# Row sums through the right matrix in groups of eight, with the output products eleven turns behind a row's first stage

## The chip, the cores and the metric

The kernel runs on one core of a Trainium2 chip. The metric is the device time of one execution in microseconds (us). The engines are TensorE (PE; its weight loads are listed apart as PEld), VectorE (DVE), ScalarE (ACT), GpSimd (POOL) and SyncE (SP), which here only issues transfers. Everything is in 32-bit floats.

## What is computed

The input x has 384 x 384 positions of 128 channels. Two layers follow each other; the first mixes rows, the second works row by row. Cut to what matters:

```
# layer 0
z     = layernorm(x)
left  = (z @ Wl + bl) * sigmoid(z @ Wlg + blg)
right = (z @ Wr + br) * sigmoid(z @ Wrg + brg)
core  = einsum('bikh,bjkh->bijh', left, right)
x1    = x + sigmoid(x @ Wg + bg) * (layernorm(core) @ Wout + bout)
# layer 1
left  = x1 @ W_left + b_left + x1 @ W_eq + b_eq
gate  = sigmoid(x1 @ W_gate + b_gate)
rsum  = sum over j of (x1 @ W_right + b_right)      # one vector of 128 per row i
out   = layernorm((left * rsum * gate) @ W_out + b_out + x1)
```

The sum over j and the product with W_right can change places. So the kernel adds up each row of x1 first (one vector of 128 per row) and sends only these sums through W_right. It also multiplies rsum into W_out, which gives each row an output matrix of its own.

## The kernel before

It works in three stages. Stage 1 normalises x, forms left and right and writes them to memory. Stage 2 forms core, channel by channel. Stage 3 begins with the first transposes at about 1888 us and does the end of layer 0 and all of layer 1, one row i of 384 positions at a time. Only stage 3 is touched.

In stage 3 the channels lie on the 128 partitions and the 384 positions of a row along the free dimension. The order on every engine is the order in which the program writes the instructions (`seq` keeps it)[...]. The main loop runs over turns t (L610 to L644). In each turn different functions work on different rows, so that each engine finds its inputs ready:

- `front(f)` (L488) runs ahead. It forms the gate gT of row f-2 (matmul "pg" L493, sigmoid on ACT L495), and every fourth row asks for the x of four rows by a transfer, 16 rows ahead (L499). At the start it is up to 14 rows ahead of t, later 2. For the first 24 rows x is transposed on TensorE ("pxt" L506); after that it is put together in a tile "xt" by two transfers (L441, and an accumulating one that POOL issues, L449).
- `load_core` (L622) asks for core and its scaling for four rows, eight rows ahead; `scale_core(t)` (L627) multiplies them on POOL into "cs".
- `last(t-10)` (L629) multiplies by the layer norm's weight on DVE (L601) and adds its bias on POOL (L602).
- `right_sums(m)` (L631) is called in every fourth turn, t = 6, 10, 14 and so on, for rows 4m to 4m+3: one matmul "pq" (L514) of W_right with a tile "tot" of 128 x 4, which holds four rows' sums, and the addition of the bias on DVE into "rsum" (L516).
- `layer0(t-2)` (L633) is a row's first stage: matmul "pr" (L530), then two DVE instructions (L531, L533). The second writes x1T and, on the side, the row's sum into its column of "tot".
- `out_matrix(t-6)` (L635): ACT scales W_out by a column of rsum into "wo" (L541).
- `gated_left(t-3)` (L637): matmuls "pg" (L547) and "pl" (L548), sigmoid on ACT (L550), product "u" on DVE (L552).
- `layer1(t-7)` and `stats1(t-7)` (L639): the output product "py", three times a matmul of u with wo (L559) and a transpose of x1T added into it (L560); its statistics on DVE (L574, L576). After every second row POOL turns the statistics of two rows into a scale and a shift (L578 to L583).
- `norm1(t-9)` (L642) normalises on ACT (L590), and every fourth turn `store` (L644) writes four rows out.

After the loop L646 to L663 finish the last four rows.

The TensorE order in a turn is therefore: pg (and pxt) of `front`, pq in every fourth turn, pr, the gate and left products, py. Results of TensorE go into PSUM banks: four of them, taken in rotation by pr, pq, pg, pl and pxt (`bank`), and four more for py. The x1T and u tiles have 7 buffers each (pool "p3l", L616), the x tiles 7 of four rows each (pool "p3x", L416).

Of the kernel before, what the change touches and what calls it, by code (L numbers as in the profile page):

```python
# [8 lines left out]
F32 = mybir.dt.float32  # L9
AF = mybir.ActivationFunctionType  # L10
ALU = mybir.AluOpType
# [3 lines left out]
P = 128  # L15
# [4 lines left out]
def triangle_then_gated_row_kernel(ctx: ExitStack, tc: tile.TileContext, a: dict, out: bass.AP):  # L20
# [12 lines left out]
    nc = tc.nc  # L33
    x = a["x"].rearrange("b i j c -> (b i) j c")
    y = out.rearrange("b i j c -> (b i) j c")
    N, _, C = x.shape
# [7 lines left out]
    RG = 4  # L44
    A = 14
# [10 lines left out]
    def seq(ins):  # L56

        return tc.keep_in_program_order(ins)
# [21 lines left out]
    with ExitStack() as ctx2:  # L80
        lrp = ctx2.enter_context(tc.tile_pool(name="lr", bufs=2))
        inp = [ctx2.enter_context(tc.tile_pool(name="p2in", bufs=2))]
# [13 lines left out]
        with tc.tile_pool(name="p1x", bufs=6, side="right") as xp, \  # L96
# [74 lines left out]
            def after(kind, name):  # L171

                shape, view = ([P, 1], "(p o) -> p o") if kind == "col" else ([P, P], None)
                t = const(shape, kind + "_" + name)
                later.append((t, a[name].rearrange(view, o=1) if view else a[name]))
                return t
# [6 lines left out]
            wright, bright = after("mat", "L1_conv_W_right"), after("col", "L1_conv_b_right")  # L183
# [67 lines left out]
            def front(n, q, z):  # L251

                pt = tps.tile([P, 4, P], F32, tag="pt", name="pt")
                for r in range(4):
                    seq(nc.tensor.transpose(pt[:, r, :], z[:, r, :], ident))
                zt = zts[n, q] = ztp.tile([P, 4, P], F32, tag="zt", name="zt")
                seq(nc.scalar.copy(zt, pt))  # L257
# [101 lines left out]
        with tc.tile_pool(name="p2more", bufs=1, side="right", reuse_waits="tile") as more, \  # L359
# [10 lines left out]
            right = {}  # L370
# [15 lines left out]
            for h in range(H):  # L386
                fill(h + 1)
                t, rr = loaded2.pop(h), right.pop(h)
                pc = ps.tile([P, NB, 512], F32, tag="pc", name="pc")
                for kb in range(NB):  # L390
                    for ib in range(NB):
                        seq(nc.tensor.matmul(  # L392
                            pc[:, ib, :N], lhsT=t[:, kb, ib * P:(ib + 1) * P, 0], rhs=rr[:, kb],
                            start=(kb == 0), stop=(kb == NB - 1),
# [17 lines left out]
    with ExitStack() as ctx3:  # L412
        def pool(name, bufs, **kw):
            return ctx3.enter_context(tc.tile_pool(name=name, bufs=bufs, reuse_waits="tile", **kw))

        xp, fp, inp, op = pool("p3x", 7), pool("p3f", A + 4), pool("p3in", 3), pool("p3out", 3)  # L416
        wp, sp, late = pool("p3w", 4), pool("p3s", 4), []
        ps, ps2 = pool("p3ps", 4, space=PSUM), pool("p3ps2", 4, space=PSUM)

        def bank(name):  # L420
            return ps.tile([P, 512], F32, tag="bank", name=name)

        def work(name, pool=wp):
            return pool.tile([P, N], F32, tag=name, name=name)
# [4 lines left out]
        rows, yts, pair, quad, xin, xts, cin = {}, {}, {}, {}, {}, {}, {}  # L429
# [24 lines left out]
        def load_core(i0):  # L454
            if i0 < N:
                ct = inp.tile([P, RG, N], F32, tag="ct", name="ct")
                seq(nc.sync.dma_start(out=ct, in_=core_d[i0:i0 + RG].rearrange("i h j -> h i j")))
                rt = inp.tile([P, RG, N], F32, tag="rt", name="rt")
                seq(nc.sync.dma_start(
                    out=rt.rearrange("p i j -> p (i j)"),  # L460
                    in_=rstd_d[i0:i0 + RG].rearrange("i j -> (i j)").partition_broadcast(P),
                ))
                cin[i0] = ct, rt
# [19 lines left out]
                seq(nc.vector.scalar_tensor_tensor(r, r, 1.5, m, ALU.add, ALU.mult))  # L483
                seq(nc.gpsimd.dma_start(out=rstd_d[b * P:(b + 1) * P, :], in_=r))

        D = 10

        def front(f):  # L488

# [17 lines left out]
                    seq(nc.scalar.copy(xT, pxt[:, :N]))  # L507
                rows[f] = {"xT": xT}

        def right_sums(m):  # L510

            q = quad[m]
            pq = bank("pq")
            seq(nc.tensor.matmul(pq[:, :4], lhsT=wright, rhs=q["tot"], start=True, stop=True))  # L514
            q["rsum"] = sp.tile([P, 4], F32, tag="rsum", name="rsum")
            seq(nc.vector.tensor_scalar(q["rsum"], pq[:, :4], bright, None, ALU.add))  # L516

        def scale_core(i):
            ct, rt = cin[i // RG * RG]
# [3 lines left out]
        def layer0(i):  # L523

            r = rows[i]
            m, n = divmod(i, 4)
            if n == 0:
                quad[m] = {"tot": sp.tile([P, 4], F32, tag="tot", name="tot")}
            pr = bank("pr")
            seq(nc.tensor.matmul(pr[:, :N], lhsT=wc, rhs=r["cs"], start=True, stop=True))  # L530
            seq(nc.vector.scalar_tensor_tensor(pr[:, :N], pr[:, :N], bz, r["gT"], ALU.add, ALU.mult))  # L531
            x1T = r["x1T"] = work("x1T", late[0])
            seq(nc.vector.scalar_tensor_tensor(  # L533
                x1T, pr[:, :N], bout1, r["xT"], ALU.add, ALU.add, accum_out=quad[m]["tot"][:, n:n + 1]
            ))

        def out_matrix(i):

            wo = rows[i]["wo"] = wp.tile([P, C], F32, tag="wo", name="wo")
            m, n = divmod(i, 4)  # L540
            seq(nc.scalar.activation(wo, wout1, AF.Copy, scale=quad[m]["rsum"][:, n:n + 1]))  # L541

        def gated_left(i):
# [10 lines left out]
        def layer1(i, py):  # L554

            r = rows[i]
            r["py"] = py
            for s in cols:
                seq(nc.tensor.matmul(py[:, s], lhsT=r["u"][:, s], rhs=r["wo"], start=True, stop=False))  # L559
                seq(nc.tensor.matmul(  # L560
                    py[:, s], lhsT=r["x1T"][:, s], rhs=ident, start=False, stop=True, is_transpose=True
                ))

        def stats1(i):

            py = rows[i]["py"]
            m, n = divmod(i, 2)
            if n == 0:
                pair[m] = [sp.tile(s, F32, tag=k, name=k) for k, s in
                           (("mv", [P, 2, NB, 2]), ("rs", [P, 2, NB]), ("nm", [P, 2, NB]))]  # L570
            mv, rs, nm = pair[m]
            st = sp.tile([P, NB, 6], F32, tag="st", name="st")
            for b in range(NB):
                seq(nc.vector.bn_stats(st[:, b, :], py[:, cols[b]]))  # L574
            for b in range(NB):
                seq(nc.vector.bn_aggr(mv[:, n, b, :], st[:, b, :]))  # L576
            if n == 1:
                seq(nc.gpsimd.tensor_scalar(rs, mv[:, :, :, 1], EPS, 1.0, ALU.add, ALU.mult))  # L578
                seq(nc.gpsimd.tensor_tensor(  # L579
                    rs, rs, mhalf[:, :2 * NB].rearrange("p (a b) -> p a b", b=NB), ALU.pow  # L580
                ))
                seq(nc.gpsimd.tensor_tensor(nm, mv[:, :, :, 0], rs, ALU.mult))
                seq(nc.gpsimd.tensor_scalar(rs, rs, -1.0, 0.0, ALU.mult, ALU.add))  # L583

        def norm1(i):
            m, n = divmod(i, 2)
            mv, rs, nm = pair[m]
            py = rows[i]["py"]
            for b, s in enumerate(cols):
                seq(nc.scalar.activation(  # L590
                    py[:, s], py[:, s], AF.Identity, bias=nm[:, n, b:b + 1], scale=rs[:, n, b:b + 1]
                ))

        def last(i):

            i0, n = i // RG * RG, i % RG
            if n == 0:
                yts[i] = op.tile([P, RG, NB, C], F32, tag="yt", name="yt")
            yt = yts[i0][:, n]
            py = rows.pop(i)["py"]  # L600
            seq(nc.vector.tensor_tensor(yt, py[:, :N].rearrange("p (b c) -> p b c", b=NB), lnsb, ALU.mult))  # L601
            seq(nc.gpsimd.tensor_tensor(yt, yt, lnbb, ALU.add))  # L602

        def store(i0):
            seq(nc.sync.dma_start(out=y[i0:i0 + RG].rearrange("i (b p) c -> p i b c", p=P), in_=yts.pop(i0)))
# [4 lines left out]
        for t in range(N + 3):  # L610

            while f < min(N + 2, t + max(2, A - t // 3)):
                if f == 6:
                    rstd()
                    end2.close()
                    late.append(pool("p3l", 7, side="right"))  # L616
                    load_core(0)
                    load_core(RG)
                front(f)
                f += 1  # L620
            if t % RG == 0:
                load_core(t + 2 * RG)  # L622
            if added <= f + 8:
                add_x(added)
                added += RG
            if t < N:
                scale_core(t)  # L627
            if t >= D:
                last(t - D)  # L629
            if t >= 6 and (t - 6) % 4 == 0:  # L630
                right_sums((t - 6) // 4)  # L631
            if 2 <= t < N + 2:
                layer0(t - 2)  # L633
            if t >= 6:
                out_matrix(t - 6)  # L635
            if t >= 3:
                gated_left(t - 3)  # L637
            if t >= 7:
                layer1(t - 7, ps2.tile([P, 512], F32, tag="py", name="py"))  # L639
                stats1(t - 7)  # L640
            if t >= 9:
                norm1(t - 9)  # L642
            if t >= D and (t - D) % RG == RG - 1:
                store(t - D - RG + 1)  # L644

        for i in range(N - 3, N):  # L646
            out_matrix(i)
# [45 lines left out]
```

## Time and profile before

The time before is 3333.22 us, the median of 3 runs (3332.3 to 3334.1). The profiled execution spans 3331.8 us with a mean granted TensorE clock of 0.996. The costliest groups of stage 3, over the whole run:

| line | engine | what | count | busy us | mean ns of one |
|---|---|---|---|---|---|
| L559 | PE | py, u with wo, 128 columns | 2304 | 403.0 | 275 |
| L530 | PE | pr, 384 columns | 768 | 318.9 | 497 |
| L560 | PE | py, transpose of x1T | 1152 | 314.0 | 273 |
| L548 | PE | pl, 384 columns | 768 | 311.6 | 488 |
| L547 | PE | pg of the gate, 384 columns | 768 | 311.4 | 487 |
| L590 | ACT | normalise py | 1152 | 494.3 | 429 |
| L521 | POOL | cs | 384 | 405.0 | 1059 |
| L602 | POOL | yt | 384 | 403.9 | 1052 |

The profile counts two TensorE instructions for each 32-bit matmul with its weight load and one for each transpose, so 384 rows give 768 pr and 2304 py. The records of neighbouring matmuls overlap, so their busy times add up to more than the time that they take. A line of the timeline gives the start of a run of instructions, how long it lasts, engine, line, operation, what is written and read, shapes, and how many there are; the brackets at its end give the engine's idle time before it and who ended it.

### The profile page before, as it was taken

How to read it: one execution, taken by the hardware profiler on the slowest of the kernel's cores; microseconds unless marked ns; L12 is line 12 of the kernel's file. 1: busy time of each engine (PE TensorE's matmuls, PEld its weight loads, DVE VectorE, ACT ScalarE, POOL GpSimd, SP SyncE). 2: the span in 40 equal slices, each digit the busy share in tenths (PEclk: the TensorE clock that was granted, in tenths of full speed). 3: DMA queues.
4: the chain of work that ended last, by engine and by line, in shares of the span. 5: the costliest groups of instructions: out<-in, count | busy, mean ns of one | idle time of the engine just before them, and what ended most of it. 6: DMA issues, size and time to landing. Idle time of an engine off the chain costs nothing.

```text
span 3331.8 us, 48534 instructions
## 1 busy us (share of the span) xinstructions
PE 3283.0 (99%) x12584; PEld 2004.5 (60%) x12584; DVE 2503.8 (75%) x8074; ACT 1949.2 (59%) x4049; POOL 2250.2 (68%) x3267
## 2 busy tenths in 40 slices
PE   8999999999999999999999999999999999999997
PEld 4444444444444566666666567777777777777775
DVE  6777777777777655555555678888888888888887
ACT  4455555555555433333334467777777777777776
POOL 5555555555555465565566468888888888888887
PEclk9999999999999999999999999999999999999999
DMA  5899899999999498998999988889888988988883
GB/s 148 245 282 281 253 282 275 260 281 269 266 281 263 149 282 283 284 282 282 284 282 284 277 257 249 271 274 275 266 272 273 272 269 273 276 268 270 273 269 95
DMA packets 924619, 872.93 MB, mean 262 GB/s; under 512 B 24868, under 2 KB 839720, under 8 KB 924344
## 3 DMA queue, kind: packets, MB, share of 16 engines
q1 hardware_dynamic: 904960, 794.32, 76.2%
q0 software_dynamic: 13152, 71.37, 10.5%
q10 hardware_dynamic: 6232, 4.13, 0.4%
q8 instruction: 103, 1.69, 0.2%
q14 instruction: 172, 1.41, 0.1%
HBM read 507.85 MB, written 361.89 MB: 261 GB/s over the span
## 4 chain that ended last, share of the span: by engine, by line
PE 62%; ACT 1%; POOL 1%; DVE 0%; issue 0%; DMA 0%; POOLq 0%; SPq 0%; ACTq 0%
PE pc L392 22%; PE pr L530 7%; PE py L559 7%; PE pg L493 7%; PE pl L548 7%; PE pg L547 7%; PE py L560 4%; ACT py L590 1%; POOL rs L579 0%; PE pq L514 0%; DMA xt<-nd_d 0%; POOL yt L602 0%; PE pxt L506 0%; DVE yt L601 0%; DVE st L574 0%
## 5 line engine op out<-in xcount | busy, mean ns | idle before, releaser
L291 PE MATMUL pr<-wz,zt 128*128 128x512 f32 x2304 | 1042.8, 594 | 0.7 <-ACT zt L257 0.7
L298 ACT ACTIVATE sg<-pr,rs 128x256 f32<-128x256 f32 x1152 | 482.8, 470 | 507.8 <-PE pr L291 375.1
L392 PE MATMUL pc<-rr,lrh 128*128 128x384 f32 x2304 | 743.3, 486 | 1.9 <-DVE lr L300 1.9
L300 DVE SCALAR_TENSOR_TENSOR lr<-pr,rs,sg 128x256 f32<-128x256 f32 x1152 | 504.8, 480 | 274.8 <-ACT sg L298 226.9
L291 PEld LDWEIGHTS pr<-wz,zt 128*128 128x128 f32 x2304 | 415.3, 191 | 412.5 <-issue 346.9
L392 PEld LDWEIGHTS pc<-rr,lrh 128*128 128x128 f32 x2304 | 452.0, 196 | 293.2 <-issue 2.5
L590 ACT ACTIVATE py<-py,nm,rs 128x128 f32<-128x128 f32 x1152 | 494.3, 429 | 184.4 <-POOL rs L583 90.8
L559 PEld LDWEIGHTS py<-wo,u 128*128 128x128 f32 x2304 | 377.5, 191 | 102.4 <-ACT wo L541 1.7
L401 DVE TENSOR_TENSOR csum<-csum,ct 128x1152 f32<-128x1152 f32 x128 | 180.6, 1411 | 343.0 <-ACT ct L398 343.0
L521 POOL TENSOR_TENSOR cs<-ct,rt 128x384 f32<-128x384 f32 x384 | 405.0, 1059 | 2.8 <-PE pr L530 2.6
L398 ACT COPY ct<-pc 128x1152 f32<-128x1152 f32 x128 | 143.2, 1118 | 450.5 <-PE pc L392 450.5
L602 POOL TENSOR_TENSOR yt<-yt,lnb 128x384 f32<-128x384 f32 x384 | 403.9, 1052 | 2.9 <-DVE yt L601 2.6
L559 PE MATMUL py<-wo,u 128*128 128x128 f32 x2304 | 403.0, 275 | 1.2 <-ACT wo L541 1.2
L378 POOL COPY rr<-lrh 128x768 f32<-128x768 f32 x128 | 184.8, 1444 | 298.6 <-DMA lrh<-lr_d 287.4
L574 DVE BATCH_NORM_STATS2 st<-py 128x6 f32<-128x128 f32 x1152 | 266.1, 286 | 96.0 <-PE py L560 95.3
L246 POOL TENSOR_TENSOR z<-xt,nd 128x512 f32<-128x512 f32 x288 | 299.8, 1041 | 43.4 <-POOL z L246 30.0
L530 PE MATMUL pr<-cs,wc 128*128 128x384 f32 x768 | 318.9, 497 | 5.4 <-POOL cs L521 5.4
L236 POOL TENSOR_SCALAR sd<-mv 128x8 f32<-128x8 f32 x144 | 28.4, 197 | 436.5 <-DVE mv L225 436.4
L560 PE MATMUL py<-ident,x1T 128*128 128x128 f32 x1152 | 314.0, 273 | 0.0
L548 PE MATMUL pl<-x1T,mat_L_conv_W_left 128*128 128x384 f32 x768 | 311.6, 488 | 1.2 <-ACT gT L495 1.2
L547 PE MATMUL pg<-x1T,mat_L_conv_W_gate 128*128 128x384 f32 x768 | 311.4, 487 | 1.0 <-DVE x1T L533 0.6
L493 PE MATMUL pg<-xt,mat_L_conv_Wg 128*128 128x384 f32 x720 | 292.0, 487 | 0.0
(96 smaller groups left out, 4919.6 us busy)
## 6 DMA issues: line engine op xcount, KB each, us to landing
lr_d<-lr SPq DMA_DIRECT2D x128, 1024.0 KB, 7.2
lrh<-lr_d SPq DMA_DIRECT2D x128, 768.0 KB, 7.7
xt_d<-zt SPq DMA_DIRECT2D x288, 256.0 KB, 5.5
ct<-core_d SPq DMA_DIRECT2D x96, 768.0 KB, 6.4
rt<-rstd_d SPq DMA_DIRECT2D x96, 768.0 KB, 8.1
out_dram<-yt SPq DMA_DIRECT2D x95, 768.0 KB, 4.9
core_d<-ct SPq DMA_DIRECT2D x125, 576.0 KB, 8.6
xt<-in_x_dram SPq DMA_DIRECT2D x140, 512.0 KB, 6.8
```

The lines of the kernel that those rows point to most:

```text
L291: seq(nc.tensor.matmul(pr[:, r, :], lhsT=zts[n, q][:, 2 * half + r, :], rhs=wz, start=True, stop=True))
L298: seq(nc.scalar.activation(sg[r], pr[:, r, 2 * H:], AF.Sigmoid, scale=rs[r]))
L300: seq(nc.vector.scalar_tensor_tensor(t[:, :, c * XR + r0 + r, :], pr[:, r, :2 * H].rearrange("k (h s) -> k h s", s=2), rs[r], sg[r].rearra ...
L392: seq(nc.tensor.matmul(pc[:, ib, :N], lhsT=t[:, kb, ib * P:(ib + 1) * P, 0], rhs=rr[:, kb], start=(kb == 0), stop=(kb == NB - 1),))
L493: seq(nc.tensor.matmul(pg[:, :N], lhsT=wg0, rhs=r["xT"], start=True, stop=True))
L521: seq(nc.gpsimd.tensor_tensor(cs, ct[:, i % RG], rt[:, i % RG], ALU.mult))
L530: seq(nc.tensor.matmul(pr[:, :N], lhsT=wc, rhs=r["cs"], start=True, stop=True))
L547: seq(nc.tensor.matmul(pg2[:, :N], lhsT=wgate, rhs=r["x1T"], start=True, stop=True))
L548: seq(nc.tensor.matmul(pl[:, :N], lhsT=wleft, rhs=r["x1T"], start=True, stop=True))
L559: seq(nc.tensor.matmul(py[:, s], lhsT=r["u"][:, s], rhs=r["wo"], start=True, stop=False))
L560: seq(nc.tensor.matmul(py[:, s], lhsT=r["x1T"][:, s], rhs=ident, start=False, stop=True, is_transpose=True))
L590: seq(nc.scalar.activation(py[:, s], py[:, s], AF.Identity, bias=nm[:, n, b:b + 1], scale=rs[:, n, b:b + 1]))
```

## The change

The row sums are now sent through W_right eight rows at a time, by a matmul of 128 x 8, so that there are fewer of these small matmuls. The first row of a group then has to wait for seven more rows before its rsum exists, so everything from `out_matrix` on moves from seven turns behind to eleven. In the last 48 rows the groups are of four, and at rows 337, 345, 353 and 361 one row joins the turn of the row ahead of it, so that the output products are seven turns behind again at the end and the code after the loop stays as it is. A table made ahead of the loop holds the group of each row (`group`), the turns in which sums are formed (`sums`) and the turn of each row's output product (`turn`, `at`). The x1T and u tiles get 11 buffers in place of 7 to live longer, and the x tiles 6 in place of 7, which makes room for them.

```diff
-        xp, fp, inp, op = pool("p3x", 7), pool("p3f", A + 4), pool("p3in", 3), pool("p3out", 3)
+        xp, fp, inp, op = pool("p3x", 6), pool("p3f", A + 4), pool("p3in", 3), pool("p3out", 3)
...
-        D = 10
+        firsts = list(range(0, N - 48, 8)) + list(range(N - 48, N, 4))
+        group, sums, turn = {}, {}, []
+        for i0, i1 in zip(firsts, firsts[1:] + [N]):
+            sums[i1 + 2] = i0, i1
+            for i in range(i0, i1):
+                group[i] = i0, i - i0
+                t = turn[-1] + 1 if i else 0
+                turn.append(max(i1 + 3, t - (i0 >= N - 48 and i % 8 == 1 and t > i + 7)))
+        assert turn[N - 5:] == list(range(N + 2, N + 7))
+        at = {t: [i for i in range(N) if turn[i] == t] for t in range(N + 7)}
...
-            seq(nc.tensor.matmul(pq[:, :4], lhsT=wright, rhs=q["tot"], start=True, stop=True))
-            q["rsum"] = sp.tile([P, 4], F32, tag="rsum", name="rsum")
-            seq(nc.vector.tensor_scalar(q["rsum"], pq[:, :4], bright, None, ALU.add))
+            seq(nc.tensor.matmul(pq[:, :i1 - i0], lhsT=wright, rhs=q["tot"][:, :i1 - i0], start=True, stop=True))
+            q["rsum"] = sp.tile([P, 8], F32, tag="rsum", name="rsum")
+            seq(nc.vector.tensor_scalar(q["rsum"][:, :i1 - i0], pq[:, :i1 - i0], bright, None, ALU.add))
...
-                    late.append(pool("p3l", 7, side="right"))
+                    late.append(pool("p3l", 11, side="right"))
...
-            if t >= D:
-                last(t - D)
-            if t >= 6 and (t - 6) % 4 == 0:
-                right_sums((t - 6) // 4)
+            done = at.get(t - 3, [])
+            for i in done:
+                last(i)
+            if t in sums:
+                right_sums(*sums[t])
             if 2 <= t < N + 2:
                 layer0(t - 2)
-            if t >= 6:
-                out_matrix(t - 6)
+            for i in at[t + 1]:
+                if i < N - 3:
+                    out_matrix(i)
             if t >= 3:
                 gated_left(t - 3)
-            if t >= 7:
-                layer1(t - 7, ps2.tile([P, 512], F32, tag="py", name="py"))
-                stats1(t - 7)
-            if t >= 9:
-                norm1(t - 9)
-            if t >= D and (t - D) % RG == RG - 1:
-                store(t - D - RG + 1)
+            for i in at[t]:
+                layer1(i, ps2.tile([P, 512], F32, tag="py", name="py"))
+                stats1(i)
+            for i in at.get(t - 2, []):
+                norm1(i)
+            for i in done:
+                if i % RG == RG - 1:
+                    store(i - RG + 1)
```

More of the change, by code (lines that the diff above doesn't have):

```diff
@@ L508, in front, with right_sums @@
                 rows[f] = {"xT": xT}
-        def right_sums(m):
-            q = quad[m]
+        def right_sums(i0, i1):
+            q = quad[i0]
             pq = bank("pq")
-            seq(nc.tensor.matmul(pq[:, :4], lhsT=wright, rhs=q["tot"], start=True, stop=True))
-            q["rsum"] = sp.tile([P, 4], F32, tag="rsum", name="rsum")
-            seq(nc.vector.tensor_scalar(q["rsum"], pq[:, :4], bright, None, ALU.add))
+            seq(nc.tensor.matmul(pq[:, :i1 - i0], lhsT=wright, rhs=q["tot"][:, :i1 - i0], start=True, stop=True))
+            q["rsum"] = sp.tile([P, 8], F32, tag="rsum", name="rsum")
+            seq(nc.vector.tensor_scalar(q["rsum"][:, :i1 - i0], pq[:, :i1 - i0], bright, None, ALU.add))
         def scale_core(i):
@@ L525, in layer0 @@
             r = rows[i]
-            m, n = divmod(i, 4)
+            m, n = group[i]
             if n == 0:
-                quad[m] = {"tot": sp.tile([P, 4], F32, tag="tot", name="tot")}
+                quad[m] = {"tot": sp.tile([P, 8], F32, tag="tot", name="tot")}
             pr = bank("pr")
@@ L539, in out_matrix @@
             wo = rows[i]["wo"] = wp.tile([P, C], F32, tag="wo", name="wo")
-            m, n = divmod(i, 4)
+            m, n = group[i]
             seq(nc.scalar.activation(wo, wout1, AF.Copy, scale=quad[m]["rsum"][:, n:n + 1]))
```

## The prediction, on record before the changed kernel ran

> **What bounds the kernel now.** I read the page's engine shares first, then the busy time of the third stage alone, TensorE's waits in it, and TensorE's timeline over two turns. A turn is one pass of the loop over t; "pr" of one turn to "pr" of the next is its length. The page's part 1 and chain by engine:
>
> ```profile
> PE 3283.0 (99%) x12584; PEld 2004.5 (60%) x12584; DVE 2503.8 (75%) x8074; ACT 1949.2 (59%) x4049; POOL 2250.2 (68%) x3267
> ...
> PE 62%; ACT 1%; POOL 1%; DVE 0%; issue 0%; DMA 0%; POOLq 0%; SPq 0%; ACTq 0%
> ```
>
> TensorE is busy for 99% and holds nearly all of what the chain names. The third stage, which alone is changed, runs from 1913.4 us (first pr) to the end. Busy time in its even part:
>
> ```profile
> core 0: us, PE busy (x) PEld busy (x) DVE busy (x) ACT busy (x) POOL busy (x), PEclk, DMA share, GB/s
> 1960.00:3300.00 1340.00, 1338.80 (x6456) 948.15 (x6455) 1178.10 (x4160) 977.21 (x2210) 1146.38 (x1567) 1.00 0.87 263
> ```
>
> PE idles 1.2 us in 1340; DVE is busy 88%, POOL 86%, ACT 73%, the transfers 87%. TensorE's waits from 1960 to 3304 us are one line (waiter, whom for, us in all, times, longest):
>
> ```profile
> PE pl L548 <- ACT gT L495: 1.2, 2, 0.6
> ```
>
> So here TensorE's own queue is the time, and an instruction taken off it shortens the stage, if it cost its queue anything. The small product pq (right_sums, L514) has its own view:
>
> ```profile
> L514 PEld LDWEIGHTS pq<-tot,mat_L_conv_W_right x192: 186/190/192, 1928.6 to 3305.4; 128*128 128x128 f32 x192
> L514 PE MATMUL pq<-tot,mat_L_conv_W_right x192: 169/248/253, 1928.7 to 3305.4; 128*128 128x4 f32 x192
> L516 DVE TENSOR_SCALAR rsum<-pq,col_L_conv_b_right x96: 210/211/214, 1929.1 to 3307.8; 128x4 f32<-128x4 f32 x96
> ...
>   ACT wo L541: 26.0, 94
> ```
>
> It runs 96 times, each as two weight loads and two matmuls (min/median/max ns). Only ScalarE's wo waits for it. Its cost is not the 248 ns record; it is what it adds between starts. TensorE's timeline, a turn without pq and the next one with it (start, us, line):
>
> ```profile
> 2604.76 0.81 PE L493 MATMUL pg<-xt,mat_L_conv_Wg 128*128 128x384 f32 x2
> 2605.41 0.81 PE L530 MATMUL pr<-cs,wc 128*128 128x384 f32 x2
> 2606.05 0.81 PE L547 MATMUL pg<-x1T,mat_L_conv_W_gate 128*128 128x384 f32 x2
> ...
> 2607.34 0.38 PE L559 MATMUL py<-wo,u 128*128 128x128 f32 x2
> ...
> 2608.34 0.81 PE L493 MATMUL pg<-xt,mat_L_conv_Wg 128*128 128x384 f32 x2
> 2608.99 0.28 PE L514 MATMUL pq<-tot,mat_L_conv_W_right 128*128 128x4 f32 x2
> 2609.13 0.89 PE L530 MATMUL pr<-cs,wc 128*128 128x384 f32 x2
> 2609.86 0.81 PE L547 MATMUL pg<-x1T,mat_L_conv_W_gate 128*128 128x384 f32 x2
> 2611.14 0.38 PE L559 MATMUL py<-wo,u 128*128 128x128 f32 x2
> ```
>
> py to py is 2607.34 - 2603.77 = 3.57 us without pq and 2611.14 - 2607.34 = 3.80 us with it. It splits in two: pq to pr is 0.14 us, and pr to the next product 0.73 instead of 0.64. Over the stage I took pr to pr of all turns: median 3.578 us in 272 turns without pq at their end, 3.717 us in 90 with one (+0.139), and 3.66 us in the turn that begins behind one (+0.083). **One pq costs 0.222 us of TensorE's queue**, four columns wide.
>
> [...] records of 0.81 us start every 0.645 us. So I count starts. [...] In the trace the pair before pq loads under the 384-column matmul before it; pq's four columns are too short to cover the two loads that follow. Hence the cost is loads without cover, and eight columns should cost about the same.
>
> **The change part by part.**
>
> *Fewer pq.* The rows are grouped in eights up to row 336 (42 groups) and in fours to 384 (12): 54 pq in place of 96. 42 x 0.222 = 9.3 us off TensorE's queue, all on the path. Rsum on DVE goes 42 times by 0.21 us, off the path.
>
> *Wider pq.* A 384-column matmul starts its successor 322 ns later, 0.84 ns a column; 4 columns x 2 matmuls x 42 x 0.84 = 0.3 us at most, zero if covered by the loads. I take 0.3.
>
> *Lag 11 in place of 7.* Each row's py, stats, norm, last and store keep their distances among themselves and move four turns back. x1T and u get 11 buffers instead of 7, so a buffer is written again two turns after py read it, as before (t = i+13 against i+11). Nothing new to wait for. The pq stands one turn behind the last x1T of its group, as before.
>
> *Start.* Turns 7 to 10 lose their py set (2608.34 - 2607.34 = 1.00 us each), which is run later. That costs nothing if TensorE stays full without it. Two such turns can be seen in the trace: the one from 1928.87 took 2.99 us, just its products plus the 0.08 behind a pq; the one from 1926.37 (without pg) took 2.50 where its products and pq sum to 2.07, an excess of 0.42. Bounds: 0 and all four sets, 4.0 us. I take 0.6.
>
> *Four double turns.* To come back from lag 11 to 7, turns 347, 354, 361 and 368 carry two rows' py: 1.00 us more TensorE work in each, the same sets that the start left out. DVE then has two rows' stats (+1.0 us on 3.16, below TensorE's 4.58). Two turns on ACT has six norms: 0.73 x 3.58 = 2.6, plus 1.35, is 3.97 us in a turn of 3.58. Queued behind on ACT are the next gT and g2; DVE's u, its next pr and x1T wait for them, and TensorE's next gate product waits for x1T. Three turns on DVE has a second yt (+0.56) and POOL too (+1.06). Between x1T and the gate product that reads it the trace shows 1.2 us (x1T begun 3301.27 and done near 3301.9; product 3303.07), about what the later norm takes. Bounds: 0, and a full 1.0 us each, 4.0. I take 0.2 each, 0.8. py has four PSUM buffers; the second py of a double turn needs the yt of the same turn, which DVE runs first (3300.15 to 3300.71, py at 3301.43): no wait.
>
> *Six x tiles in place of seven.* Tile f+16 is asked for in turn f-1 and its buffer was last read by row f-5's layer0 in turn f-3. The issue waits at SP, with core loads and stores queued behind, only if DVE is over two turns late. The core loads stand eight turns ahead (28.6 us) of a landing of 6.4 to 8.1 us (page, part 6). Early, where front runs ahead, one load (row 48) is asked for a turn before its buffer is free; the core load behind it keeps seven turns. Cost 0, hidden by that lead.
>
> *Fewer late banks.* The one wait of TensorE above comes in turns with a pq, which takes a bank out of four, so pl needs the bank of the same turn's pg, whose gT was late:
>
> ```profile
> 1986.92 0.57 ACT L495 ACTIVATE gT<-pg,col_L_conv_bg 128x384 f32<-128x384 f32 x1
> ...
> 1987.55 0.91 PE L548 MATMUL pl<-x1T,mat_L_conv_W_left 128*128 128x384 f32 x2 [0.56 <-ACT gT L495]
> ```
>
> Two turns (4.49 from 1985.5, 4.57 from 2027.4) are 0.83 and 0.91 us above 3.66. With half the pq there I count half: -0.9.
>
> *The end* keeps its order: the last rows are in fours at lag 7.
>
> Sum: -9.3 + 0.3 + 0.6 + 0.8 - 0.9 = -8.5; 3333.2 - 8.5 = **3324.7 us**.
>
> **The rivals.**
> 1. *More comes off*: start and doubles cost nothing and both late banks go: -9.3 - 1.7 = 3322.2. For it: PE has hardly a wait. Against: the excess of 0.42 at the start is real.
> 2. *The moved work isn't free*: turns 7 to 10 run at the pace of the chain cs, pr, x1T (TensorE idles 2.0 and 3.3 us for cs at 1913 and 1921), and doubles stall 0.5 us each: -9.3 + 4.0 + 2.0 = 3329.9. Against: from turn 5 on the trace has no such wait for cs.
> 3. *Slower*: with transfers at 87%, and one x tile less, SP issues late and 96 core loads each hold up cs and TensorE by 0.2 us, +19.2: 3333.2 - 9.3 + 19.2 = 3343. Against: the eight turns of lead. Only a wait at SP longer than 20 us would show.
>
> **How the numbers follow.** Forecast 0.70 (3323.3 to 3326.5); rival 1, 0.10; rival 2, 0.14 (3326.5 to 3331); rival 3, 0.06. The bound of 0.2% is 6.7 us, 3326.5. Faster: 0.70 + 0.10 + 0.01 = 0.81; within: 0.13; slower: 0.06. Range 3322.2 to 3328.5: its low end is rival 1, its high end takes in half of rival 2.
>
> **What would show it.** 54 pq, each adding about 0.22 us; pr to pr still 3.578 in turns without one; TensorE's waits from 1960 on still under 2 us; the four double turns near 4.58 and the turns behind them at 3.58. Wrong if turns 7 to 10 show gaps on TensorE, if the turns two or three behind a double grow, if PE waits for cs or a transfer, or if a pq eight wide costs more than 0.23.

## The result, and the profile after

The changed kernel takes 3323.76 us (median of 6 runs, 3321.82 to 3325.41) beside 3333.66 us (3332.14 to 3336.23, 6 runs) of the kernel before: a ratio of 0.997, 95% interval 0.9957 to 0.9983. The forecast was 3324.7 us. Two later comparisons of the same two kernels gave 0.9968 (0.9957 to 0.998) and 0.9969 (0.9957 to 0.9981). The change makes the kernel faster by 0.3%, some 10 us.

The page after, part 1 and the chain by engine:

```profile
PE 3270.4 (99%) x12500; PEld 1993.7 (60%) x12500; DVE 2497.6 (75%) x8032; ACT 1947.4 (59%) x4049; POOL 2250.4 (68%) x3267
...
PE 63%; POOL 1%; DVE 1%; ACT 1%; issue 0%; DMA 0%; POOLq 0%; DVEq 0%; ACTq 0%
```

TensorE has 84 instructions fewer (12584 - 12500), two for each of 42 small products, and DVE 42. The engine that bounds the kernel is the same. The busy times of the even part of stage 3 (columns as in the line of before):

```profile
1960.00:3288.00 1328.00, 1326.65 (x6379) 938.26 (x6378) 1171.30 (x4127) 975.43 (x2215) 1150.20 (x1571) 1.00 0.88 265
```

TensorE idles 1.35 us in 1328. POOL's share goes from 86% (1146.38 of 1340) to 87% (1150.20 of 1328), since the same work stands in less time. TensorE's waits from 1960 to 3292 us are again a single line:

```profile
PE pl L560 <- ACT gT L507: 1.3, 2, 0.8
```

The view of pq, whose lines are now L526 and L528:

```profile
L526 PEld LDWEIGHTS pq<-tot,mat_L_conv_W_right x108: 186/190/192, 1937.4 to 3293.4; 128*128 128x128 f32 x108
L526 PE MATMUL pq<-tot,mat_L_conv_W_right x108: 169/214/256, 1937.5 to 3293.5; 128*128 128x8 f32 x84, 128*128 128x4 f32 x24
L528 DVE TENSOR_SCALAR rsum<-pq,col_L_conv_b_right x54: 210/216/225, 1937.8 to 3295.8; 128x8 f32<-128x8 f32 x42, 128x4 f32<-128x4 f32 x12
```

There are 54 of them, 42 eight wide. The first comes at 1937.5 us, behind turn 9, and no longer at 1928.7. From pr to pr, a turn that ends with a pq takes 3.718 us (3.717 before), the one that begins behind it 3.66, and one without 3.578: none of these lengths has changed, only the number of turns with a pq. A double turn on TensorE's timeline, from 3149.02 to 3153.60 us:

```profile
3149.02 0.81 PE L542 MATMUL pr<-cs,wc 128*128 128x384 f32 x2
...
3150.96 0.38 PE L571 MATMUL py<-wo,u 128*128 128x128 f32 x2
...
3151.95 0.39 PE L571 MATMUL py<-wo,u 128*128 128x128 f32 x2
...
3152.95 0.81 PE L505 MATMUL pg<-xt,mat_L_conv_Wg 128*128 128x384 f32 x2
3153.60 0.81 PE L542 MATMUL pr<-cs,wc 128*128 128x384 f32 x2
```

The first row's py takes from 3150.96 to 3151.95, the second row's from there to 3152.95: no bracket for an idle engine, and the turn is 4.58 us, 3.578 + 1.00. So the turn costs just the second row's own products, and these are the ones that the start left out.

**Where the 10 us are.** I compared each turn with the spacing of its own products (0.645 us for 384 columns, 0.326 for a set of pxt, 1.00 for a set of py, 0.222 for pq) and call the rest its excess. The profiles are two of before and three of after. From pr of turn 4 (before at 1921.66 and 1922.14 us, after at 1921.90, 1923.39 and 1922.56) to the last pr, before takes 1380.77 and 1380.93 us, after 1368.59, 1370.29 and 1369.12: a mean difference of 11.5 us. It is made of (in us):

| part | predicted | measured |
|---|---|---|
| 42 small products | -9.3 | -9.3 |
| eight columns in place of four | +0.3 | 0.0 |
| start, turns 5 and 10 | +0.6 | -1.1 |
| start, TensorE's clock in turn 4 | none | -0.9 |
| four double turns and those behind them | +0.8 | +0.2 |
| late banks, turns 15 to 42 | -0.9 | -0.2 |
| other turns | 0 | -0.1 |

Up to pr of turn 4 the two kernels differ by what the first transfers do; there the after profiles are 0.7 us later on the mean. So at the last pr after is ahead by 10.8 us. From there both need the same 29.4 us (3331.8 - 3302.43; 3319.9 - 3290.49).

### The profile page after: what moved, and what is told of

Its sections match the earlier page's. It is cut to its first block, busy times and chain, and to the rows that moved or that the text cites. A ratio compares the mean times of both kernels' runs of the same rounds, so it can differ in the third digit from the quotient of the medians.

```text
span 3319.9 us, 48372 instructions
## 1 busy us (share of the span) xinstructions
PE 3270.4 (99%) x12500; PEld 1993.7 (60%) x12500; DVE 2497.6 (75%) x8032; ACT 1947.4 (59%) x4049; POOL 2250.4 (68%) x3267
## 4 chain that ended last, share of the span: by engine, by line
PE 63%; POOL 1%; DVE 1%; ACT 1%; issue 0%; DMA 0%; POOLq 0%; DVEq 0%; ACTq 0%
PE pc L392 22%; PE pr L542 7%; PE py L571 7%; PE pl L560 7%; PE pg L559 7%; PE pg L505 7%; PE py L572 4%; ACT py L602 0%; POOL rs L591 0%; PE pq L526 0%; POOL yt L614 0%; DMA rt<-rstd_d 0%; POOL cs L533 0%; DMA rstd_d<-r 0%; DVE yt L613 0%
```

## The experiments

**The same two kernels again.** No edit; the question is how much of the start is chance.

> The kernel before once more, unchanged, for the spread of the third stage's start. Theory A (the start's excess is chance: how long the first transfers take and where the TensorE clock drops): ratio to before 1.000, and the excess of turns 2 to 12 over their products differs from the first profile's 7.7 us by 1 us or more. Theory B (the start's excess belongs to the kernel): 7.7 us again within 0.5.

Measured: 3333.97 us beside 3334.08, ratio 0.9999 (0.9991 to 1.0008). Excess of turns 2 to 12: 7.71 us again (first profile 7.67).

> The changed kernel once more. Theory A (chance): its excess in turns 2 to 12 differs from the first profile's 4.5 us by 1 us or more, and may come near that of before; from turn 13 on its turns are as in the first profile. Theory B (the change itself shortens the start by 3 us): 4.5 us again within 0.5. Time by both about 3324 us, 0.997 of before.

> The changed kernel beside it, on the same chip, for the comparison: 3323 to 3324 us, 0.997 of before; loop 1376 to 1378 us; the clock drop of turn 4 (1.8 us of excess) may come or not.

Measured: 3322.74 us, ratio 0.9968 (0.9957 to 0.998), and 3323.14 us beside 3333.58, ratio 0.9969 (0.9957 to 0.9981). Excess of turns 2 to 12: 5.67 and 4.27 us, against 4.48 in the first profile. Most of that spread is turn 4, with an excess of 0.11, 1.79 and 0.73 in the three profiles. Its products on the timeline of the second profile:

```profile
1923.39 0.91 PE L542 MATMUL pr<-cs,wc 128*128 128x384 f32 x2 [2.45 <-POOL cs L533]
1924.14 0.95 PE L559 MATMUL pg<-x1T,mat_L_conv_W_gate 128*128 128x384 f32 x2
1924.88 1.48 PE L560 MATMUL pl<-x1T,mat_L_conv_W_left 128*128 128x384 f32 x2
1926.16 1.48 PE L505 MATMUL pg<-xT,mat_L_conv_Wg 128*128 128x384 f32 x2
```

After 2.45 us of waiting for cs, pl and pg stand 1.28 us apart, twice the usual 0.64: the granted clock is 0.50 from 1924.67 to 1928.09 us. The first profile shows the same products at 0.64 after a wait of 2.22 us. It has a stretch of clock 0.50 too, but earlier, from 1913.52 to 1916.93, in turns 2 and 3. The slow stretches here last 3.41 us, or twice that (1917.21 to 1924.04 in the third profile). In the first profile TensorE did nothing in the 3.41 us ahead of the slow stretch, but in the second it was busy for 1.28 of them (1921.26 to 1924.67), and the clock fell all the same. What brings a slow stretch on was not shown.

The four profiles with a wait of 3.3 to 3.5 us ahead of turn 4 (both of before, "the small product twice" and "at the head of its turn" below) all have their slow stretch there (1922.28 to 1925.68 us in the first of before) and show 1.8 us of excess in it. In the other eight the wait is shorter, from none to 2.7 us, and that excess runs from 0 to 1.79. In turn 3 a slow stretch need not cost anything, since TensorE waits for cs there in any case: with one from 1915.68 to 1919.10 ("the small product once") turn 3 has 4.03 us of excess, and 4.43 without one in before. So the -0.9 of the table hangs on where the slow stretch falls. How far the wait for the first transfers decides that was not shown. Whether the change itself moves it isn't settled. Outside turns 2 to 4 the profiles of one kernel agree within 0.3 us.

**Lag and buffers alone.** On the changed kernel:

```diff
-        firsts = list(range(0, N - 48, 8)) + list(range(N - 48, N, 4))
+        firsts = list(range(0, N, 4))
-                t = turn[-1] + 1 if i else 0
+                t = turn[-1] + 1 if i else 11
```

> One part alone: lag 11, 11 buffers of x1T and u, six x tiles and the four double turns, but the sums in fours as before (96 small products). My theory (the gain is the 42 small products, and the moved output products cost nothing): same as before within 1.5 us, about 3333 us; double turns 4.58 us. Rival 1 (the lag itself gives something, by starting without the output products or by fewer late banks): 3330 us or less. Rival 2 (lag and double turns cost, and hide a larger gain of the eights): 3335 us or more.

Measured: 3333.1 us, ratio 0.9997 (0.9989 to 1.0006). All that surrounds the small products, the lag, 11 buffers, six x tiles and four double turns, moves the time by nothing that can be told from zero: the medians differ by 1.0 us, and the interval reaches from 3.7 us less to 2.0 more. The changed kernel took 3322.74 us beside it, so the gain is the eights. Turn by turn, this kernel also shows the two small parts of the start apart. From 1925 to 1950 us TensorE's waits before are:

```profile
PE pg L547 <- ACT gT L495: 0.4, 1, 0.4
PE pq L514 <- DVE x1T L533: 0.2, 1, 0.2
```

With lag alone only the second stays. The first is turn 10, where ACT's first norms stood ahead of gT; with the lag they come four turns later. The second, turn 5 and 0.42 us of excess in all, is a pq with nothing ahead of it but the product it depends on; in the changed kernel its first pq stands behind a pg and three transposes, and both waits are gone. Together they are the -1.1 of the table. The double turns are as in the changed kernel: 4.575 us, and 0.17 us of excess three turns behind the first of them.

**The small product twice.** On the kernel before, the matmul of `right_sums` is issued a second time into the same bank.

```diff
             seq(nc.tensor.matmul(pq[:, :4], lhsT=wright, rhs=q["tot"], start=True, stop=True))
+            seq(nc.tensor.matmul(pq[:, :4], lhsT=wright, rhs=q["tot"], start=True, stop=True))
```

> The kernel before with every small product issued twice into the same bank, so 192 in place of 96. Theory A (each costs 0.222 us of TensorE's queue, mostly two weight loads without cover): 96 x 0.222 = 21.3 us slower, 3355 us, 1.0064 of before; the turn with two of them ends 0.36 us over 3.578. Theory B (the cost is the wait for its input or a bank, not the loads): the second finds all ready and costs under 0.1 us, under 10 us in all.

Measured: 3353.83 us, ratio 1.0058 (1.0041 to 1.0075), 19.8 us slower. TensorE's timeline:

```profile
2604.02 0.28 PE L514 MATMUL pq<-tot,mat_L_conv_W_right 128*128 128x4 f32 x2
2604.16 0.36 PE L515 MATMUL pq<-tot,mat_L_conv_W_right 128*128 128x4 f32 x2
2604.38 0.89 PE L531 MATMUL pr<-cs,wc 128*128 128x384 f32 x2
2605.11 0.81 PE L548 MATMUL pg<-x1T,mat_L_conv_W_gate 128*128 128x384 f32 x2
```

The second has its input and its bank, and still puts 2604.38 - 2604.16 = 0.22 us between itself and pr. Theory B falls: the cost isn't a wait. The weight loads of the same stretch point to what it is:

```profile
2603.70 0.51 PEld L514 LDWEIGHTS pq<-tot,mat_L_conv_W_right 128*128 128x128 f32 x2
2604.13 0.30 PEld L515 LDWEIGHTS pq<-tot,mat_L_conv_W_right 128*128 128x128 f32 x2
2604.36 0.30 PEld L531 LDWEIGHTS pr<-cs,wc 128*128 128x128 f32 x2
2604.79 0.51 PEld L548 LDWEIGHTS pg<-x1T,mat_L_conv_W_gate 128*128 128x128 f32 x2
```

A pair of loads with a 384-column matmul running between their starts lasts 0.51 us: 0.32 between the starts and 0.19 for the second load's record. The pairs of the second pq and of pr last 0.30, so their loads start 0.11 apart, and pr's pair starts 2604.36 - 2604.13 = 0.23 us behind that of the second pq. Here one load follows another every 0.11 us, with only a product of four columns to run beside them. A turn with two ends after 3.941 us, 0.224 more than with one. 96 x 0.224 is 21.5; 0.9 us of it come back as shorter waits in the two late turns (0.40 and 0.46 us of excess in place of 0.83 and 0.91), since there TensorE waits for ACT in any case. The profiled spans differ by 20.5 us (3352.3 - 3331.8).

**The small product once.** On the kernel before; it leaves out the row sums of all rows but the first four:

```diff
-            if t >= 6 and (t - 6) % 4 == 0:
+            if t == 6:
...
-            seq(nc.scalar.activation(wo, wout1, AF.Copy, scale=quad[m]["rsum"][:, n:n + 1]))
+            seq(nc.scalar.activation(wo, wout1, AF.Copy, scale=quad[0]["rsum"][:, n:n + 1]))
```

> The kernel before with a single small product, for the first four rows, whose rsum serves all rows (so the row sums of all later rows are left out; lag, buffers and x tiles as before). Theory A (each small product is worth 0.222 us of TensorE's queue, and nothing else of the change matters): 95 x 0.222 = 21.1 us off, and the two late banks of 0.9 us go too: 3311 to 3313 us, 0.9935 of before. Theory B (when they go, another engine sets the pace): turns stay above 3.578 us and less than 15 us come off.

Measured: 3310.29 us beside 3333.86, ratio 0.993 (0.9915 to 0.9945), 23.6 us less: the 21.1 of 95 products, and the rest from the late turns (0.9 us less excess in turns 15 to 42) and from turn 4, which ran at full clock here. Turns without pq still take 3.578 us, 362 of them, so no other engine has taken over, even with all small products but one gone. In turns 15 to 42 about 1 us of excess stays, now in turns 27, 31, 33 and 37: about half of that loss doesn't need a pq. What the change takes off is 42/95 of what was there.

**The small product at the head of its turn.** The changed kernel with the call of `right_sums` ahead of `front`.

```diff
+            if t in sums:
+                right_sums(*sums[t])
             while f < min(N + 2, t + max(2, A - t // 3)):
...
-            if t in sums:
-                right_sums(*sums[t])
             if 2 <= t < N + 2:
```

> The changed kernel with the small product moved to the head of its turn, ahead of front's pg, so that the left product takes the bank of the small product of the same turn and no longer that of pg. Theory A (the two late turns at 1992 and 2020 us wait for pg's bank, because the small product shifts the rotation): both waits of 0.8 and 1.0 us go, 1.9 us off, 3321.5 us. Theory B (they come from POOL's accumulating transfers alone, wherever the small product stands): both stay. A small product at the head might wait for the last x1T instead: then its turns grow beyond 3.72 us.

Measured: 3322.47 us, ratio 0.9966 (0.9953 to 0.9979), the same as the changed kernel. Pl no longer waits for gT anywhere from 1930 us on, as theory A said of the bank. But pq now waits itself. These are all the waits that TensorE's view lists from 1930 to 3292 us:

```profile
PE pq L526 <- ACT py L602: 0.4, 1, 0.4
PE pq L526 <- DVE x1T L545: 0.4, 1, 0.4
```

The first is at 3176.57 us. The view names ACT there, but DVE finished the last row sum that pq reads only at 3176.42, so this too may be a wait for the sum. The excess of turns 15 to 42 goes from 1.9 to 1.0 us, and about 1.0 us of new excess appears in turn 9 and just ahead of the second double turn. One wait has been changed for another; nothing is gained.

**The first accumulating transfer later.** On the changed kernel:

```diff
-            if added <= f + 8:
+            if t >= 6 and added <= f + 8:
```

> The changed kernel with POOL's first accumulating transfer held back to turn 6. In the traces POOL waits for its input from 1914.9 to 1919.7 us in turn 2, and cs of row 2 stands behind it, so TensorE idles 2 to 3 us[...]. Theory A (this wait is the start's excess): turns 2 to 12 lose their 3.5 to 4.5 us of excess, 3318 to 3320 us. Theory B (core and scaling of the next rows arrive as late): the wait turns into one of POOL for a core transfer, and less than 1.5 us come off.

Measured: 3319.77 us (3317.98 to 3321.02), ratio 0.9958 (0.9943 to 0.9973), 3.4 us under the 3323.14 us of the changed kernel's last comparison; the changed kernel's fastest run of all three comparisons took 3321.51. POOL's timeline in the changed kernel, and then in this one:

```profile
1912.95 1.94 POOL L533 TENSOR_TENSOR cs<-ct,rt 128x384 f32<-128x384 f32 x2 [0.76 <-DMA rt<-rstd_d]
1919.89 0.93 POOL L449 DMA_DIRECT2D xt<-xt_d  x1 [5.00 <-PE pxt L518]
1920.52 5.12 POOL L533 TENSOR_TENSOR cs<-ct,rt 128x384 f32<-128x384 f32 x5
```

```profile
1912.54 3.85 POOL L533 TENSOR_TENSOR cs<-ct,rt 128x384 f32<-128x384 f32 x4 [0.43 <-DMA rt<-rstd_d]
1917.76 1.95 POOL L533 TENSOR_TENSOR cs<-ct,rt 128x384 f32<-128x384 f32 x2 [1.37 <-DMA rt<-rstd_d]
1919.84 0.93 POOL L449 DMA_DIRECT2D xt<-xt_d  x1
```

In the changed kernel POOL stands still for 5.00 us ahead of the transfer, which waits for its x tile, and cs of five rows comes behind it. Moved, the transfer starts at nearly the same moment, 1919.84, and six cs are done before it in place of two. The excess of turns 2 to 12 falls to 1.27 us. It is the one profile of all without a slow stretch there: the granted clock is 1.00 from 1905.2 to 1990 us. This is a loss that both kernels had (POOL waits 5.38 us at this place in before), and no part of the change.

**Groups of twelve.** On the changed kernel:

```diff
-        xp, fp, inp, op = pool("p3x", 6), pool("p3f", A + 4), pool("p3in", 3), pool("p3out", 3)
+        xp, fp, inp, op = pool("p3x", 6), pool("p3f", A + 4), pool("p3in", 3), pool("p3out", 2)
-        firsts = list(range(0, N - 48, 8)) + list(range(N - 48, N, 4))
+        firsts = list(range(0, N - 48, 12)) + list(range(N - 48, N, 4))
-                turn.append(max(i1 + 3, t - (i0 >= N - 48 and i % 8 == 1 and t > i + 7)))
+                turn.append(max(i1 + 3, t - (i0 >= N - 48 and i % 4 == 1 and t > i + 7)))
-                    late.append(pool("p3l", 11, side="right"))
+                    late.append(pool("p3l", 15, side="right"))
```

and "tot" and "rsum" of twelve columns.

> Groups of twelve up to row 336 and of four after it, lag 15, 15 buffers of x1T and u, two output tiles in place of three for room, eight double turns, four rows apart: 40 small products in place of 54. If a small product costs 0.222 us at any width and the moved work nothing: 14 x 0.222 = 3.1 us less than the changed kernel, 3320.5 us. If double turns four apart stall (DVE, ACT and POOL each get over a turn's work twice in a row) or two output tiles hold up yt: 3324 us or more.

Measured: 3319.59 us (3319.23 to 3320.78), ratio 0.9958 (0.9944 to 0.9972). From the first pr to the last it takes 1373.41 us; the changed kernel's three profiles are 1376.49, 1377.69 and 1376.18, so 3.4 us less on the mean. That is near 14 x 0.222 = 3.1 in part by luck. Eight double turns four rows apart do begin to cost: 0.92 us of excess from turn 333 on, in place of 0.2. And the start was shorter: 3.84 us of excess in turns 2 to 12, 1.0 less than the changed kernel's mean. 3.1 - 0.7 + 1.0 is the 3.4.

**Both together.** Groups of twelve and the later transfer.

> Both together on the changed kernel: groups of twelve (40 small products) and POOL's first accumulating transfer in turn 6. If the two terms are of different stretches they add up: the loop from first pr to last is 3.1 us shorter by the small products and 2.5 to 4.4 us by the start than the changed kernel's 1376.5 to 1377.7 us, so 1369 to 1371 us, and the time 3316 to 3318 us. If the start's gain is spent elsewhere: 3319 us or more.

Measured: 3318.33 us (3316.88 to 3318.79), ratio 0.9952 (0.994 to 0.9965). All its five runs lie below all six of the changed kernel beside it (3322.93 to 3323.76), so it is faster than both kernels. It is a little short of what was expected: from first to last pr it takes 1372.03 us and not 1369 to 1371. In this profile turns 2 and 3 have 2.56 us of excess where the later transfer alone had 1.24; the granted clock is 0.50 from 1914.81 to 1918.23. The changed kernel's start varies as much between its profiles.

## Why the prediction was right

**Fewer pq: right, and it is the gain.** The price of 0.222 us, read from starts of neighbouring products and not from the record of 248 ns, held from both sides: doubling the product costs 0.224 us each, and leaving 95 out gives what 95 x 0.222 and the late turns predict. The weight loads of a turn of before show where they stand:

```profile
2608.23 0.30 PEld L493 LDWEIGHTS pg<-xt,mat_L_conv_Wg 128*128 128x128 f32 x2
2608.66 0.51 PEld L514 LDWEIGHTS pq<-tot,mat_L_conv_W_right 128*128 128x128 f32 x2
2609.10 0.30 PEld L530 LDWEIGHTS pr<-cs,wc 128*128 128x128 f32 x2
```

The first load of pq begins 0.32 us behind the start of pg at 2608.34 and 0.33 ahead of pq's own at 2608.99, so it runs beside pg; pr's pair begins 0.11 us behind that start, with only pq beside it. That the cost is two weight loads without cover was an estimate of mine. It is supported by the doubled product, which waits for nothing and is followed by the same 0.22 us, by its loads, which start 0.11 us apart there, and by the width, which did not matter. The loads were not changed by themselves.

**Wider pq: +0.3 taken, 0.0 measured.** The +0.3 was taken as the most that it could be, with zero named as possible; four more columns show no cost.

**Lag 11: right.** No new waits; lag alone is 0.9997 of before.

**Start: the sign was wrong.** I priced turns 7 to 10 without py at +0.6, from the 0.42 us of excess in the turn at 1926.37. Those turns ran with 0.02 us of excess. The 0.42 didn't belong to a turn without py, but to its pq, which waited for the x1T just made; the later first pq took it away. Pq's own view has the line for it, a wait of 0.2 us for x1T, and I put the loss down to the wrong thing. For the 0.7 of turn 10 the sum has no term. Together -1.1.

**Double turns: +0.8 taken, +0.2 measured.** The overload of ACT is there. Its timeline two turns behind the double:

```profile
3159.15 2.63 ACT L602 ACTIVATE py<-py,nm,rs 128x128 f32<-128x128 f32 x6
3161.71 0.57 ACT L507 ACTIVATE gT<-pg,col_L_conv_bg 128x384 f32<-128x384 f32 x1
```

Six norms run back to back, and gT follows late; TensorE loses 0.17 us in the turn that follows, the third behind the double. This is one of the signs that I had named for being wrong, though a small one. Both rows of this pair have their statistics in the same turn, so the norms don't wait for POOL and begin 2.0 us after that turn's pr. Norms that wait for POOL begin 2.9 us after it (3151.89 behind the pr of 3149.02). These 0.9 us give back part of the 1.3 us that the second row's norms take. At the other three doubles nothing is lost at all; why they differ stays open.

**Late banks: the step that failed.** Halving the pq was to halve the two late turns, -0.9; the excess of turns 15 to 42 went from 2.00 and 2.15 us to 1.90, 1.92 and 1.80. The late turns moved from 22 and 34 to 26 and 34, since pq now comes in turns 10, 18, 26, 34. With the product at the head of the turn pl no longer waits, so the bank is the link for that wait. That there are still two is a matter of which turns the pq meets, so a count in proportion was no ground for the number. Nor is the pq the whole cause: with a single pq in the kernel about 1 us of the 2 is still lost in these turns. What makes gT late there was not settled.

The misses partly cancel: start, doubles and width came 2.6 us better than priced, banks 0.7 worse, and the clock in turn 4 brought 0.9 that had no price. Against that the changed kernel reached turn 4 0.7 us later. So it is in part luck that the sum lies within 1 us of the measured time. Rival 2 fell with turns 7 to 10 full, and rival 3 with no TensorE wait for cs after turn 4. Rival 1 was right that start and doubles cost next to nothing, but it also counted on the late banks, which stayed; all three medians (3323.76, 3322.74, 3323.14) lie between its 3322.2 and the forecast.

## What to carry to other kernels

Price a small matmul in a full TensorE queue by how far it moves its neighbours' starts, with and without it; here 0.22 us for four columns as for eight. So merging these products paid in proportion to their count. What surrounds them could be moved at no cost that showed while TensorE stayed full and the catching-up turns were few (0.2 us lost with four of them, 0.9 with eight). A wait at the start of a stage should be traced to the instruction that waits before it is priced as a property of the whole turn. A cheap instruction that waits can cost a good part of what the change under study gains, if others stand behind it on its engine. Here POOL stood still for 5.00 us ahead of a transfer whose issue took 0.93 us, with cs of five rows behind it, and moving it by four turns gave a third of what the 42 products gave.

## What the runs showed of the hardware that was not expected

The same kernel in the same place can run TensorE at half pace or not: pl to pg 0.64 us apart in one profile and 1.28 in the next, after waits of 2.22 and 2.45 us. In eleven of the twelve profiles a stretch of granted clock 0.50, 3.41 us long or twice that, begins between 1913 and 1925 us. Where TensorE is full it costs up to 1.8 us, which is as much as several of the terms above; where TensorE waits anyway it can cost nothing. In the 3.41 us ahead of one such stretch TensorE was idle throughout; ahead of another it was busy for 1.28 us.
